# A third pause for every two scatters of gated copies, and a new weight for the stream that holds them

## The chip, the cores and the metric

The kernel runs on one core of a Trainium2 chip. The core has TensorE (PE: matmuls, with weight loads shown as PEld), VectorE (DVE), ScalarE (ACT), GpSimd (POOL) and SyncE (SP, which here only issues DMAs). Every engine works through its own instructions in order and waits on semaphores for the others. The metric is the time of one execution on the device in microseconds; the time of a kernel is the median of its runs.

## The reference, cut to what matters

Two layers over 16 x 256 tokens of 512 channels. The first is attention over blocks, a layer norm and a gated feed-forward in quantised weights; the second is a causal convolution over time, a router that picks two of eight experts for each token, and the experts.

```python
def _L0_ffn_ref(x, w1, w2, w3):
    h = jax.nn.silu(bitlinear(x, w1)) * bitlinear(x, w2)
    return bitlinear(h, w3)

def _L1_ffn_ref(x, Wr, We, be):
    logits = jnp.einsum('bsd,de->bse', x, Wr)
    w, sel = jax.lax.top_k(logits, K_TOP)          # K_TOP = 2
    w = jax.nn.softmax(w, axis=-1)
    E = We.shape[0]
    gate = jnp.einsum('bsk,bske->bse', w, jax.nn.one_hot(sel, E, dtype=w.dtype))
    out = jnp.zeros(x.shape[:2] + (We.shape[2],), dtype=x.dtype)
    for e in range(E):
        out = out + gate[..., e:e + 1] * (jnp.einsum('bsd,df->bsf', x, We[e]) + be[e])
    return out

x = x + _L0_ffn_ref(_L0_cond_ref(x, ...), L0_ffn_w1, L0_ffn_w2, L0_ffn_w3)
x = x + _L1_ffn_ref(_L1_cond_ref(x, cond_2048[:, None, :]), L1_ffn_Wr, L1_ffn_We, L1_ffn_be)
```

## The kernel before

**Tiling.** The 4096 tokens are cut into four blocks of 1024. A block is one tile of 128 partitions with eight rows of 512 channels in each (`X[n]`, two buffers, so that block n + 2 can be loaded only when block n is no longer read). The first layer goes row set by row set: 32 tiles m of 128 tokens, eight to a block.

**The streams.** Work is written as Python generators. Each `yield` is a pause: between two of them lies one step. The function `together` takes generators, each with a number of steps, and always advances the one whose share of steps done is smallest. So the number given with a generator is a weight: half the number makes it run twice as fast beside the others. It need not be its true number of steps.

- `ffn` is the first layer. A tile m takes six steps: four quarters of the gated product (`glu`: eight matmuls at L445, the SiLU at L450, the product at L451), after the first quarter a step with the down projection of tile m - 2 (`down`: sixteen matmuls at L487, L492), and a last step with the row quantisation (`quant_h`: L457, L459, L462, L463, with two small GpSimd operations at L359 and L131) and the transposes of the quantised rows (L475, copied by ScalarE at L477). The layer norm of two tiles at a time (L391 on GpSimd, L392 to L408, L414 to L419, turned at L427 and L429) is in there too. Its first tile of a new block is the first reader of that block.
- `behind(n - 1)` is the second layer's front for the block before: `conv`, `route`, and then the load of block n + 1 (`load_x`, four DMAs at L156 on SP).
- `experts` are the matmuls of full tiles of 128 rows for one expert each (turned at L983, multiplied at L1035), with rows read from `routed` in memory (L974) and results added into the output by GpSimd's indirect DMAs (L947). A tile takes three steps.

`conv` has ten steps (`CONV_STEPS`): two to begin, and then eight groups, each with the transposes (L675) and ScalarE's copy (L677) of the next group, 24 matmul instructions (L706) with weights loaded by SP (`taps`, L692, five buffers) and VectorE's copy of the result back into the block (L710). The accumulator comes from a pool of one bank (`ps_c`), in the tail from one of four (`ps_mm`).

`route` has nine steps of logits (transposes at L744, ScalarE's copy at L746, matmuls at L755), one with the choice of experts and of slots (L760 to L807, small operations of VectorE) and the table of tiles (`listing`), and then sixteen steps, one for each of eight rows and two chosen experts. Each of them makes a gated copy of the row (L819, ScalarE), appends four numbers (L823 on GpSimd, in the tail L821 on ScalarE) and scatters it by an indirect DMA from GpSimd (L824). The copies have three buffers (`pay`), in the tail they share twelve with other rows. In front of row 4 the table is multiplied out (L931) and cast (L936).

**The sections.** There are four. For n = 1, 2, 3 `behind(n - 1)` runs beside 48 steps (`STEPS`) of the first layer and, from n = 2 on, beside the experts of earlier blocks; n = 1 also has eight steps that load the experts' weights. In these sections `behind` is given `behind_steps * 7 // 4` as its weight, where `behind_steps = CONV_STEPS + ROUTE_STEPS` = 10 + 26 = 36. For n = 4, the tail, the first layer is done: convolution, logits and choice are stepped through without a partner, and the sixteen scatters run beside twelve tiles of experts (36 steps), with `behind_steps - head` as their number of steps, head being 20. Behind them come the last partial tiles of experts, which read rows of all scatters, and the final sum.

**The order.** What the streams set is the order in which instructions are written down. It is not yet the order on the engines: the instructions are then put in order by when they are ready as well, and the written order says which of several ready ones goes first.

## Time and profile before

| | us |
|---|---|
| median of 3 runs (lowest, highest) | 1011.78 (1010.33, 1012.91) |
| profiled execution | 1019.93 |
| its span, first to last instruction | 1018.0 |
| TensorE busy | 886.0 (87%) |
| VectorE busy | 570.2 (56%) |
| ScalarE busy | 484.1 (48%) |
| GpSimd busy | 315.6 (31%) |

The page gives busy times of the engines in the span, their shares of 40 equal slices, the costliest groups of instructions and the chain of work that ended last. A busy TensorE is not a TensorE at its peak, since matmuls are pipelined and their ends are modelled. The slices show where TensorE, ScalarE and GpSimd are busy, and the clock granted to TensorE:

```profile
PE   3678898798988899987998999879969998999992
...
ACT  2797765664577674456665515665511240111110
POOL 0135210323046312017434111462121045454541
PEclk9788998899999999999999999999989889999996
```

A slice is 25.45 us, a digit is tenths of it. The three sections lie at about 219 to 371, 371 to 561 and 561 to 747 us, the tail behind them. Of the groups, the scatters:

```profile
L824 POOL DMA_INDIRECT routed<-pay,slot x64 | 63.7, 995 | 42.6 <-issue 9.3
```

This reads: 64 instructions at line 824 on GpSimd, from `pay` and `slot` to `routed`, together 63.7 us busy, 995 ns in the mean, and GpSimd idle for 42.6 us in all just ahead of them.

### The profile page before, as it was taken

The page shows a single profiled execution, that of the slowest core. Times are in us where ns is not written, and L with a number is a line of the kernel's source. Part 1 is how long each engine was busy: PE and PEld are TensorE (multiplying, and loading weights), DVE is VectorE, ACT ScalarE, POOL GpSimd, SP SyncE. Part 2 cuts the span into 40 slices and gives each one's busy share as a digit, 9 for nine tenths or more (in the row PEclk, how much of TensorE's full clock was granted, in tenths as well). Part 3 has the DMA queues.
Part 4 walks back from the last instruction along what each step waited for, and adds up shares of the span by engine and source line. Part 5 has one row for each costly group of instructions (what it writes and reads, how often), then busy time and mean ns, then how long its engine had stood idle before and what let it go on. Part 6 is the DMA issues. An engine that isn't in the chain of part 4 may idle for free.

```text
span 1018.0 us, 13482 instructions
## 1 busy us (share of the span) xinstructions
PE 886.0 (87%) x4456; PEld 500.5 (49%) x4456; DVE 570.2 (56%) x1243; ACT 484.1 (48%) x635; POOL 315.6 (31%) x383
## 2 busy tenths in 40 slices
PE   3678898798988899987998999879969998999992
PEld 1223443357743467653443776435438944544440
DVE  3799864878385986454678543645513262333234
ACT  2797765664577674456665515665511240111110
POOL 0135210323046312017434111462121045454541
PEclk9788998899999999999999999999989889999996
DMA  9970100865226034325531642362579077877767
GB/s 331 356 263 0 60 21 7 283 230 159 63 84 225 26 102 157 95 66 173 166 84 19 191 146 63 105 197 63 109 221 273 17 216 214 219 176 193 180 162 241
DMA packets 73547, 151.56 MB, mean 149 GB/s; under 512 B 9276, under 2 KB 26044, under 8 KB 72840
## 3 DMA queue, kind: packets, MB, share of 16 engines
q1 hardware_dynamic: 57384, 108.93, 32.1%
q0 software_dynamic: 15440, 39.20, 16.3%
q10 hardware_dynamic: 656, 2.58, 0.8%
q8 instruction: 36, 0.59, 0.2%
q14 instruction: 31, 0.25, 0.1%
HBM read 96.50 MB, written 54.18 MB: 148 GB/s over the span
## 4 chain that ended last, share of the span: by engine, by line
PE 54%; DVE 13%; ACT 10%; DMA 9%; issue 7%; POOL 6%; SPq 0%; DVEq 0%; POOLq 0%; ACTq 0%
PE acc_ps L1035 19%; PE acc_ps L445 10%; PE acc_ps L706 7%; PE acc_ps L487 6%; PE acc_ps L755 3%; PE acc_ps L983 3%; DMA routed<-pay,slot 3%; ACT hq L457 2%; DVE h L451 2%; ACT hq L463 2%; PE acc_ps L744 2%; POOL routed L824 2%; DMA xg<-routed 2%; PE acc_ps L475 1%; DMA xt<-in_x 1%
## 5 line engine op out<-in xcount | busy, mean ns | idle before, releaser
L1035 PE MATMUL acc_ps<-we,xT 128*128 x568 | 267.3, 607 | 1.5 <-ACT h L450 1.3
L445 PEld LDWEIGHTS <-qT 128*128 128x128 bf16 x1024 | 99.6, 99 | 147.8 <-issue 42.8
L1035 PEld LDWEIGHTS acc_ps<-we,xT 128*128 128x128 f32 x568 | 105.7, 196 | 101.3 <-issue 94.7
L451 DVE SCALAR_TENSOR_TENSOR h<-acc_ps,c,h 128x512 f32<-128x512 f32 x128 | 95.2, 745 | 97.7 <-PE acc_ps L445 62.4
L445 PE MATMUL acc_ps<-w2q,qT 128*128 128x512 fp8e4 x512 | 133.6, 382 | 16.2 <-DVE h L451 8.5
L445 PE MATMUL acc_ps<-w1q,qT 128*128 128x512 fp8e4 x512 | 135.4, 384 | 8.4 <-ACT qT L429 4.1
L947 POOL DMA_INDIRECT out<-ye,oi x41 | 67.3, 1640 | 231.3 <-PE acc_ps L1035 145.4
L487 PE MATMUL acc_ps<-w3q,hqT 128*128 128x512 fp8e4 x512 | 130.2, 406 | 10.0 <-ACT w3q L217 4.6
L450 ACT ACTIVATE h<-acc_ps,c 128x512 f32<-128x512 f32 x128 | 86.3, 681 | 87.7 <-PE acc_ps L445 87.3
L986 ACT COPY xT<-acc_ps 128x512 f32<-128x512 f32 x59 | 34.4, 585 | 169.8 <-PE acc_ps L983 166.1
L706 PE MATMUL acc_ps<-taps,xT 128*128 128x128 f32 x768 | 93.1, 277 | 7.0 <-ACT xT L677 1.6
L706 PEld LDWEIGHTS acc_ps<-taps,xT 128*128 128x128 f32 x768 | 88.8, 192 | 9.9 <-ACT xT L677 2.0
L487 PEld LDWEIGHTS <-hqT 128*128 128x128 bf16 x512 | 52.3, 104 | 79.0 <-issue 26.9
L463 ACT ACTIVATE hq<-h,neg_magic 128x2048 bf16<-128x2048 f32 x32 | 64.1, 2002 | 32.7 <-DVE h L462 30.0
L824 POOL DMA_INDIRECT routed<-pay,slot x64 | 63.7, 995 | 42.6 <-issue 9.3
L459 DVE TENSOR_REDUCE hmx<-h 128x1 f32<-128x2048 f32 x32 | 73.0, 2281 | 0.6
L477 ACT COPY hqT<-acc_ps 128x1024 bf16<-128x1024 bf16 x64 | 61.9, 1009 | 17.9 <-PE acc_ps L475 16.4
L457 ACT ACTIVATE hq<-h 128x2048 bf16<-128x2048 f32 x32 | 61.2, 1912 | 16.8 <-DVE h L451 16.4
L983 PE MATMUL acc_ps<-ident,xg 128*128 128x128 f32 x284 | 45.7, 287 | 18.1 <-DMA xg<-routed 12.9
L1055 DVE SCALAR_TENSOR_TENSOR ye<-biases,xe,acc_ps 128x512 f32<-128x512 f32 x32 | 23.9, 747 | 66.3 <-PE acc_ps L1035 64.5
L983 PEld LDWEIGHTS acc_ps<-ident,xg 128*128 128x128 f32 x284 | 36.8, 150 | 45.3 <-issue 35.7
L359 POOL TENSOR_SCALAR ms<-hss 128x1 f32<-128x1 f32 x32 | 6.2, 192 | 170.0 <-ACT hq L457 169.4
(194 smaller groups left out, 1134.4 us busy)
## 6 DMA issues: line engine op xcount, KB each, us to landing
taps<-in_toep SPq DMA_DIRECT2D x128, 192.0 KB, 2.7
xg<-routed SPq DMA_DIRECT2D x71, 258.0 KB, 3.2
xt<-in_x SPq DMA_DIRECT2D x16, 512.0 KB, 8.2
we<-in_We SPq DMA_DIRECT2D x8, 1024.0 KB, 10.8
bias<-in_be SPq DMA_DIRECT2D x25, 256.0 KB, 4.0
out<-xt SPq DMA_DIRECT2D x12, 512.0 KB, 2.6
st<-in_w1T SPq DMA_DIRECT2D x4, 1024.0 KB, 12.5
st<-in_w2T SPq DMA_DIRECT2D x4, 1024.0 KB, 14.4
```

The lines of the kernel that those rows point to most:

```text
L445: nc.tensor.matmul(acc[-1], lhsT=qTs[i][:, k, bass.ts(j, P)], rhs=wq[:, k, bass.ts(f, 512)], start=(k == 0), stop=(k == KC - 1),)
L450: marks["silu", m] = nc.scalar.activation(h, acc[0], AF.Silu, scale=c1[:, j : j + 1])
L451: marks["glu", m] = nc.vector.scalar_tensor_tensor(h, acc[1], c2[:, j : j + 1], h, ALU.mult, ALU.mult)
L457: nc.scalar.activation(hq, h, AF.Square, accum_out=hss)
L459: nc.vector.tensor_reduce(hmx, h, AX.X, ALU.max, apply_absolute_value=True)
L463: nc.scalar.activation(hq, h, AF.Identity, bias=neg_magic)
L487: nc.tensor.matmul(o_ps, lhsT=hqT[k // half][:, k % half, :], rhs=w3q[:, k, :], start=(k == 0), stop=(k == KF - 1),)
L706: nc.tensor.matmul(cv_ps[:, g, :], lhsT=xT[:, g, at : at + P], rhs=mine[g][:, lag, :], start=(lag == 0), stop=(lag == LAGS - 1),)
L824: routings.append(nc.gpsimd.indirect_dma_start(out=next(rv), out_offset=bass.IndirectOffsetOnAxis(ap=slot[:, i, p : p + 1], axis=0), in_=p ...
L947: d = nc.gpsimd.indirect_dma_start(out=next(add_v), out_offset=bass.IndirectOffsetOnAxis(ap=idx, axis=0), in_=ye, in_offset=None, compute_ ...
L983: nc.tensor.transpose(xT_ps[:, k, :], xg[:, bass.ts(k, P)], ident)
L1035: last_mm = nc.tensor.matmul(e_ps, lhsT=xT[:, k, :], rhs=we[:, bass.ds(e, 1), k, :].rearrange("p o f -> p (o f)"), start=(k == 0), stop=(k ...
```

## The change

After both scatters of a row there is one more pause. So a row has three steps where it had two, in one of which nothing is issued. `ROUTE_STEPS` counts it: 26 becomes 34. Through it `behind_steps` goes from 36 to 44, its weight in the three sections from 63 to 77, and the number of steps of the scatters in the tail from 16 to 24. No instruction is added, removed or altered.

```diff
--- before.py
+++ after.py
@@ -827,7 +827,9 @@
                 ))
                 yield
 
-    ROUTE_STEPS = 1 + PH + 1 + TOP * PH
+            yield
+
+    ROUTE_STEPS = 1 + PH + 1 + (TOP + 1) * PH
```

## The prediction

> **What bounds the kernel now.** I read the page's engine shares first (TensorE busy 87%), then the times of the scatters (L824): 290.9 to 320.6, 457.3 to 488.6, 651.7 to 681 and, in the tail, 825.5 to 857.2 us. With them as boundaries I asked for the busy time of each engine by stretch. For the first of the three sections that run the first layer beside the second, and the two last stretches of the third section:

> ```profile
> core 0: us, PE busy (x) PEld busy (x) DVE busy (x) ACT busy (x) POOL busy (x), PEclk, DMA share, GB/s
> 219.00:280.00 61.00, 57.78 (x446) 46.68 (x446) 36.38 (x61) 31.32 (x42) 11.53 (x14) 1.00 0.44 139
> 280.00:322.00 42.00, 34.88 (x201) 17.49 (x202) 28.82 (x83) 33.75 (x45) 23.56 (x41) 0.96 0.33 124
> 322.00:371.00 49.00, 43.03 (x233) 20.98 (x232) 42.43 (x88) 34.15 (x44) 16.31 (x26) 0.97 0.19 67
> ...
> 641.00:683.00 42.00, 35.41 (x165) 17.60 (x166) 23.12 (x94) 28.41 (x39) 25.02 (x40) 0.92 0.49 152
> 683.00:747.00 64.00, 63.78 (x306) 31.95 (x304) 31.07 (x56) 30.40 (x35) 13.79 (x14) 1.00 0.41 94
> ```

> Convolution and logits (219 to 280) keep TensorE at 95% with ScalarE at 51%; the scatters (280 to 322) leave TensorE 7.1 us idle while ScalarE is at 80%; here the two trade places. TensorE's waits in 280 to 322 name ScalarE first:

> ```profile
> PE acc_ps L427 <- ACT hqT L477: 3.7, 2, 3.1
> PE acc_ps L445 <- DVE h L451: 1.8, 2, 1.0
> PE acc_ps L445 <- ACT h L450: 1.1, 2, 0.9
> ```

> What ScalarE does there beside the first layer is the gated copy (L819, 16 x 0.716 us = 11.1 us in a section). Its three buffers come back only when a scatter has landed; of the scatters' row, who waited for them:

> ```profile
> who waited for it (us, times):
>   ACT pay L819: 23.0, 21
> ```

> ScalarE works in order, so each such wait (16.5 us in the three sections, the rest in the tail) holds the first layer's L450 and L477 behind it. In the chain that ended last, the first section's scatters also hold the next block of x:

> ```profile
> 316.26 2.75 DMA routed<-pay,slot
> 319.12 0.73 ACT pay L819
> 319.87 5.91 DMA xt<-in_x
> ```

> The last copy frees the block, its successor is loaded at once, and GpSimd's L391 at 326.0 had waited 2.46 us for it (0.99 in the second section).

> [...] By the busy row the three scatter stretches lose 42.0-34.88, 43.0-34.96 and 42.0-35.41, in all 21.8 us. [...] I therefore multiplied the matmuls of each stretch by the undisturbed start-to-start distance of their kind in this trace (0.216 us for L445 and L487, 0.056 for L475, 0.112 for L706, 0.429 for L1035): needed 32.1, 32.4 and 31.4 us, lost 9.9, 10.6 and 10.6, in all 31.1. The same count gives 17.1 us lost in 217 us of convolution and logits (8%), and 19.6 in 183 us behind the scatters (10.7%). I use the counted figures; by the busy row the stretches behind lose 13.2 of 184 us (7.2%), the excess below would be 12.7 us, and the gain at the scatters 2.1 us in place of 2.9.

> **The change, part by part.** It adds no instruction: it moves priorities in the round-robin. The stream of the second layer is weighted by 36*7//4 = 63 before and 44*7//4 = 77 after, beside 48 steps of the first layer: 0.762 and 0.623 first-layer steps per step. A first-layer tile is 6 steps and 32 L445, 16 L487, 16 L475 and half of 8 L427 matmuls, 11.5 us, so a step is 1.92 us of TensorE.

> *Convolution and logits* are the first 20 steps: they should be through at step 15.24 before and 12.47 after, 2.77 steps or 5.3 us earlier. *Scatters* spread from 15.24-26.67 to 12.47-26.18, from 11.4 to 13.7 steps, so 20% thinner. *The load of the next x* is called at 36/63 = 44/77 = 0.571, the same place. The table's matmul and cast (L931, L936) move from 28/63 to 32/77, 1.4 steps earlier; they take under 0.5 us on their engines, and nothing waits for them in the traced stretch.

> (a) Scatters. At the 10.7% of the stretches behind them, 127 us would lose 13.6; the excess is 31.1-13.6 = 17.5 us. Copies at 1/1.2 of the density take a sixth off it: 2.9 us. Bounds: nothing, if the copies keep to their buffers' pace anyway; 5.8 us if all waits for landings go and the copies stay (16.5 of the 16.5 + 33.5 us that both fill on ScalarE, a third of the excess). I take -2.9. [...]

> (b) Next x. Copies that start 5.3 us sooner end sooner, unless the longer spread takes it back. The waits of 2.46 and 0.99 us bound the gain at 3.4; the first is on the chain. I take -2.5. What is late next is ScalarE's L463.

> (c) Convolution and logits lose cover. 16 hand-overs per section (eight of one accumulator bank to VectorE's 1.03 us copy L710, eight of transposes to ScalarE's 0.585 us copy L746) now have 1.46 us of first-layer work between them, then 1.20.

> ```profile
> L710 DVE COPY xt<-acc_ps x32: 1009/1032/1064, 224.5 to 795.8; 128x512 f32<-128x512 f32 x32
> ```

> Only what has no other matmul to put in the gap pays. TensorE's waits here are few: 3.1 us for L746 in the second section, 1.8 in the third, none there in the first. Between nothing and 48 x 0.27 = 12.8 us I take +1.5, near the row, as eight waits with 6.4 us in all name these two copies (the rest of the second and third section's are of 0.2 to 0.7 us). The DMAs go along: 32 loads of taps (192 KB each, on SP behind L706's release of five buffers) in a stretch shorter by a tenth; one wait of 1.4 us for taps stands in the third section, and may double. GpSimd's queue also carries the adds (L947, 1.6 us) and the norm's small steps (L359, L131): a scatter moved ahead of one delays it by 1 us, one that now stands behind it gives that back.

> (d) First-layer work pushed behind: under half a step net per section, 0.5 x 1.92 x 10.7% x 3 = 0.3 us; inside (c)'s margin.

> (e) Tail. Sixteen scatters go beside 36 expert steps; the second of each pair moves from 2.25 to 1.5 steps behind the first, the last of all from step 33.75 to 33. A tile takes 3.87 us, a step 1.29: 0.97 us sooner. TensorE stands 4.6 us there:

> ```profile
> 857.17 2.72 DMA routed<-pay,slot
> 860.57 3.79 DMA xg<-routed
> ```

> Between 0 and -1.0 I take -0.5, since GpSimd's adds may keep the order.

> Sum: -2.9 -2.5 +1.5 -0.5 = -4.4 us. The profiled execution took 1019.93 us (span 1018.0 and 1.9 outside), 0.8% above the median 1011.78; the share is 0.43%, so I forecast 1007.4 us.

> **Rivals.** *The pauses have no hold* (about 1011.5). Order on the engines isn't the traced order, so what is ready runs ahead:

> ```profile
> 283.43 0.44 POOL L823 COPY pay<-ends 128x4 f32<-128x4 f32 x3 [15.25 <-DVE ends L774]
> 290.89 1.22 POOL L824 DMA_INDIRECT routed<-pay,slot  x1 [7.03 <-DVE hit L850]
> ```

> The code has each L824 between two L823; three L823 ran first. In the tail ScalarE made 12 copies from 818 to 827 us, though their turns are spread over 32 us. Counting L450 on ScalarE, the copies run at first-layer steps 18 to 24 in the third section (turns 15.2 to 26.7) and 18 to 30 in the first, where the landings set the pace. Then (a) and (e) vanish, and what (b) gains (c) takes back. Against it: copies and L450 compete on ScalarE at 80%, where turn does decide.

> *The mixed stretch gets thinner* (slower, 1018). [...] If a hand-over in the order finds VectorE in L459 (2.28 us), it costs up to 2.28+1.03 us less the 0.66 us of transposes. With (c) at +9 (of 12.8) and (a), (b), (e) at half, -3, the sum is +6. It decides once the 48 hand-overs lose more than 5.9/48 = 0.12 us each on average. For it: one bank only (ps_c), and the waits for L746 are already there. Against: in the tail, convolution with no first layer runs at 3.13 us a group with 0.5 us idle in 27.

> **How the numbers follow.** A change under about 0.3% (3 us) can't be told from none here. Forecast 0.46 (near 1007, nearly all faster), no hold 0.22 (near 1011.5), thinner mix 0.32 (near 1018). Spilling at the edges gives faster 0.46, same 0.22, slower 0.32. Lower end: (a) -5.8, (b) -3.4, (e) -1 and (c) 0 make -10.2, 1001.6; a new order of instructions elsewhere may add as much as one such wait. Upper end: the thinner mix with (c) at its bound and little else, +10, 1021. The forecast's own range is 1001 to 1009.

> **What would show it.** Right: first copies some 5 us sooner in each section (283.4 before in the first), fewer than 16.5 us of ScalarE waiting for landings there, L391 no longer waiting for x. Wrong in (c): TensorE's waits for L710 and L746 growing from 6.4 us. No hold: sixteen scatters still take 30 to 34 us per section at a spacing of about 2 us. The forecast fails if the convolution doesn't move up at all, because TensorE already takes what is ready there.

## The result, and the profile after

The changed kernel took 1042.89 us (median of four runs, 1040.79 to 1050.60) beside 1012.35 for the kernel before (four runs, 1010.33 to 1014.08): 1.0288 times the time, with a 95% interval of 1.0244 to 1.0332. It is slower by about 30 us, where 1007.4 was forecast and 1021 was the upper end of the range.

The profiled execution took 1041.7 us. The head of its page (span, then busy time, share of the span and instructions of each engine):

```profile
span 1039.7 us, 13476 instructions
PE 890.3 (86%) x4456; PEld 504.6 (49%) x4456; DVE 571.6 (55%) x1243; ACT 483.1 (46%) x635; POOL 318.3 (31%) x383
```

The counts of instructions (of 13482, six fewer) and nearly all busy times are those of before; the 21.7 us of span that have come are not new work. The same stretches as in the prediction, after (columns as there; code behind L829 stands two lines lower in this kernel, so L983 and L1035 are L985 and L1037):

```profile
core 0: us, PE busy (x) PEld busy (x) DVE busy (x) ACT busy (x) POOL busy (x), PEclk, DMA share, GB/s
217.00:285.00 68.00, 62.63 (x466) 50.02 (x467) 38.98 (x75) 31.68 (x44) 10.52 (x15) 0.97 0.40 125
285.00:323.00 38.00, 28.79 (x169) 14.12 (x168) 23.96 (x69) 31.65 (x43) 22.47 (x38) 0.99 0.34 127
323.00:378.00 55.00, 46.92 (x247) 22.67 (x246) 44.74 (x91) 35.68 (x45) 18.97 (x28) 0.93 0.19 67
...
662.00:708.00 46.00, 38.14 (x169) 18.86 (x168) 25.47 (x92) 30.14 (x42) 27.46 (x44) 0.89 0.51 153
```

Convolution and logits of the first section left TensorE 3.2 us idle before (61 less 57.78) and leave it 5.4 now (68 less 62.63); the scatters left 7.1 and leave 9.2; the stretch behind them left 6.0 and leaves 8.1. The clocks of 0.93 and 0.89 in the last two rows show a second loss.

TensorE's waits over the whole run (the instruction that waited, what it waited for, us in total, times, the longest):

```profile
PE acc_ps L445 <- ACT h L450: 14.6, 11, 2.9
PE acc_ps L445 <- DVE h L451: 13.6, 11, 3.5
...
PE acc_ps L706 <- DVE xt L710: 5.8, 4, 3.2
PE acc_ps L706 <- issue: 5.7, 2, 3.7
```

Before, the four read 9.1, 10.5, 0.7 and 0.6 us. The matmuls of the convolution (L706) now wait 11.5 us in these two rows instead of 1.3 (both are waits for the bank, as the timeline below shows), and those of the first layer's gated product (L445) 28.2 instead of 19.6.

**An account that holds for every kernel here.** I took the time from the first copy L677 of the first section to that of the tail (three sections; the third ends at 770.4 us before and 796.7 after), added up TensorE's gaps of more than 150 ns, and the time at a granted clock of 0.5; the clock in this trace is either 1.0 or 0.5, and at 0.5 the matmuls start about twice as far apart (those of L445 0.427 us instead of 0.216, those of L706 0.213 instead of 0.112). Section time less the gaps less half of the half-clock time is the same in all 17 profiles, 477 to 483 us, which is the work itself:

| | three sections | TensorE gaps | time at half clock | rest |
|---|---|---|---|---|
| before | 550.7 | 55.5 | 30.7 | 479.8 |
| after | 579.0 | 71.2 | 58.0 | 478.7 |

So the 28.3 us are 15.7 us of new gaps and 13.7 us for 27.3 us more at half clock, less 1.1 of the rest. The tail, 247.7 and 243.0 us, has no part in them; it is shorter as it has 20.8 us at half clock in this profile and 34.3 in that of before. This split isn't one profile's luck. What half clock takes from a whole run is (1 - mean clock) x span; averaged over the runs it is 50 us for before (the 25 beside the first experiments) and 62 for after (four), and what is left of the span is 963 and 980 us.

By stage (convolution to the last L710 of a section, logits to the first gated copy, scatters to the end of the last L824), against the undisturbed distances between matmuls that the prediction used, convolution lost 10.6 us before and 25.5 after (its gaps 7.0 and 16.2); logits 10.8 and 6.4; scatters 26.5 and 31.9; what lies behind them 31.7 and 44.1.

**Where the convolution stands still.** The timeline of after around one of its gaps (start, duration, engine, line, operation, output and input; in brackets the idle time of the engine before it and its releaser):

```profile
409.07 1.03 PE L487 MATMUL acc_ps<-w3q,hqT 128*128 128x512 fp8e4 x4
409.36 1.42 DVE L406 SCALAR_TENSOR_TENSOR y<-y,mv,gamma 128x512 f32<-128x512 f32 x2
409.49 0.68 POOL L399 TENSOR_SCALAR ve<-mv 128x2 f32<-128x2 f32 x1 [1.62 <-DVE mv L393]
410.25 1.09 POOL L131 TENSOR_TENSOR rstd<-ve,neg_half 128x2 f32<-128x2 f32 x1
411.38 1.42 DVE L407 SCALAR_TENSOR_TENSOR y<-y,rstd,beta 128x512 f32<-128x512 f32 x2 [0.60 <-POOL rstd L131]
412.71 1.00 DVE L710 COPY xt<-acc_ps 128x512 f32<-128x512 f32 x1
...
413.81 2.55 PE L706 MATMUL acc_ps<-taps,xT 128*128 128x128 f32 x14 [3.72 <-issue]
```

The matmuls of the group before ended at 408.8, so the result could have been copied then. But L710 stands in VectorE's queue behind L406 and L407 of the layer norm, and L407 waits for GpSimd's reciprocal root (L399, L131) until 411.3. VectorE is idle for only 0.60 us of this; the rest is its own work. The copy starts at 412.7, and the one bank comes free 4.9 us after it was full. TensorE has only four matmuls of L487 and four transposes to put there; 3.72 us are left empty. The label "issue" hides this: the wait is for the bank, and the next L706 starts 0.1 us behind the copy's end. This is the gap of the second section; the first has one of 1.94 us (ended 250.0) and the third one of 3.18 (ended 619.9), and in all three L710 follows L407 and L407 the same chain over GpSimd.

The late copy is not new. The same hand-over in the second section of before:

```profile
396.86 3.62 PE L487 MATMUL acc_ps<-w3q,hqT 128*128 128x512 fp8e4 x16
397.60 1.42 DVE L406 SCALAR_TENSOR_TENSOR y<-y,mv,gamma 128x512 f32<-128x512 f32 x2
399.60 1.42 DVE L407 SCALAR_TENSOR_TENSOR y<-y,rstd,beta 128x512 f32<-128x512 f32 x2 [0.59 <-POOL rstd L131]
400.31 1.88 PE L1035 MATMUL acc_ps<-we,xT 128*128 x4
400.93 1.04 DVE L710 COPY xt<-acc_ps 128x512 f32<-128x512 f32 x1
402.03 0.60 PE L675 MATMUL acc_ps<-ident,xt 128*128 128x128 f32 x4
```

There too the bank comes free 5.0 us after it was full (at 397.0), behind the same L406 and L407. But TensorE had all sixteen matmuls of a down projection and four of the experts for that time, and no gap. Over the three sections these late hand-overs kept the bank for 3.5, 5.0 and 5.0 us before and 2.9, 4.9 and 4.7 after; TensorE had 12.0 us of other matmuls in them before and has 3.9 now. Its idle time there went from 2.1 to 8.8 us, most of what the convolution's gaps grew by. What the change took away is the cover of the one late hand-over in each section.

**What follows such a gap.** The gap of after by windows, columns as above, the clock being the one in front of the last two:

```profile
408.70:413.80 5.10, 1.40 (x9) 0.67 (x9) 4.50 (x9) 0.59 (x1) 1.77 (x2) 1.00 0.55 170
413.80:414.70 0.90, 0.89 (x8) 0.90 (x9) 0.90 (x1) 0.00 (x0) 0.00 (x0) 0.98 0.55 201
414.70:418.10 3.40, 3.40 (x19) 3.40 (x18) 0.05 (x1) 0.00 (x0) 0.00 (x0) 0.50 0.41 116
418.10:421.50 3.40, 3.40 (x16) 1.73 (x16) 1.53 (x2) 0.00 (x0) 0.00 (x0) 1.00 0.44 121
```

From 0.9 us behind the gap TensorE runs for 3.4 us at half clock, and loses another 1.7 us while it shows as fully busy. Each of the three gaps has such a window (from 250.8, 414.7 and 619.5 us; the last begins inside its gap). All half-clock stretches in the three sections of these two traces are 3.41 us long or a multiple of it: nine such windows before and seventeen after.

### The profile page after: what moved, and what is told of

It is laid out like the page before. It is cut to its first block, busy times and chain, and to the rows that moved or that the text cites. A ratio compares the mean times of both kernels' runs of the same rounds, so it can differ in the third digit from the quotient of the medians.

```text
span 1039.7 us, 13476 instructions
## 1 busy us (share of the span) xinstructions
PE 890.3 (86%) x4456; PEld 504.6 (49%) x4456; DVE 571.6 (55%) x1243; ACT 483.1 (46%) x635; POOL 318.3 (31%) x383
## 3 DMA queue, kind: packets, MB, share of 16 engines
q1 hardware_dynamic: 57384, 108.93, 32.1%
## 4 chain that ended last, share of the span: by engine, by line
PE 52%; DVE 15%; ACT 11%; issue 7%; DMA 7%; POOL 7%; SPq 0%; DVEq 0%; POOLq 0%; ACTq 0%
PE acc_ps L1037 17%; PE acc_ps L445 10%; PE acc_ps L706 7%; PE acc_ps L487 6%; DMA routed<-pay,slot 3%; PE acc_ps L755 3%; PE acc_ps L985 3%; ACT hq L457 2%; ACT hq L463 2%; DVE h L451 2%; ACT hqT L477 2%; DMA xg<-routed 2%; DVE h L462 1%; PE acc_ps L475 1%; POOL r L131 1%
## 5 line engine op out<-in xcount | busy, mean ns | idle before, releaser
L1037 PE MATMUL acc_ps<-we,xT 128*128 x568 | 264.9, 602 | 1.0 <-ACT h L450 0.8
L445 PEld LDWEIGHTS <-qT 128*128 128x128 bf16 x1024 | 100.3, 100 | 159.8 <-issue 55.2
L445 PE MATMUL acc_ps<-w2q,qT 128*128 128x512 fp8e4 x512 | 137.4, 389 | 22.9 <-DVE h L451 13.0
L1037 PEld LDWEIGHTS acc_ps<-we,xT 128*128 128x128 f32 x568 | 104.3, 193 | 98.2 <-issue 92.2
L451 DVE SCALAR_TENSOR_TENSOR h<-acc_ps,c,h 128x512 f32<-128x512 f32 x128 | 95.0, 745 | 99.3 <-PE acc_ps L445 48.5
L445 PE MATMUL acc_ps<-w1q,qT 128*128 128x512 fp8e4 x512 | 138.1, 387 | 10.9 <-ACT h L450 4.9
L450 ACT ACTIVATE h<-acc_ps,c 128x512 f32<-128x512 f32 x128 | 86.1, 681 | 116.0 <-PE acc_ps L445 115.8
L487 PE MATMUL acc_ps<-w3q,hqT 128*128 128x512 fp8e4 x512 | 128.1, 399 | 8.8 <-ACT w3q L217 5.1
L988 ACT COPY xT<-acc_ps 128x512 f32<-128x512 f32 x59 | 34.4, 585 | 170.1 <-PE acc_ps L985 167.1
L706 PE MATMUL acc_ps<-taps,xT 128*128 128x128 f32 x768 | 98.0, 286 | 15.9 <-DVE xt L710 5.8
L706 PEld LDWEIGHTS acc_ps<-taps,xT 128*128 128x128 f32 x768 | 93.8, 200 | 20.8 <-issue 7.1
L487 PEld LDWEIGHTS <-hqT 128*128 128x128 bf16 x512 | 51.6, 102 | 75.3 <-issue 20.6
L463 ACT ACTIVATE hq<-h,neg_magic 128x2048 bf16<-128x2048 f32 x32 | 64.0, 2001 | 41.2 <-DVE h L462 38.6
L824 POOL DMA_INDIRECT routed<-pay,slot x64 | 65.5, 1023 | 40.9 <-issue 10.0
L459 DVE TENSOR_REDUCE hmx<-h 128x1 f32<-128x2048 f32 x32 | 73.0, 2280 | 0.4
L457 ACT ACTIVATE hq<-h 128x2048 bf16<-128x2048 f32 x32 | 61.2, 1912 | 21.8 <-DVE h L451 21.5
L477 ACT COPY hqT<-acc_ps 128x1024 bf16<-128x1024 bf16 x64 | 61.9, 1009 | 16.6 <-PE acc_ps L475 16.5
L359 POOL TENSOR_SCALAR ms<-hss 128x1 f32<-128x1 f32 x32 | 6.1, 192 | 197.8 <-ACT hq L457 197.1
L985 PE MATMUL acc_ps<-ident,xg 128*128 128x128 f32 x284 | 44.6, 281 | 19.4 <-DMA xg<-routed 13.3
L1057 DVE SCALAR_TENSOR_TENSOR ye<-biases,xe,acc_ps 128x512 f32<-128x512 f32 x32 | 23.9, 746 | 63.8 <-PE acc_ps L1037 61.3
L985 PEld LDWEIGHTS acc_ps<-ident,xg 128*128 128x128 f32 x284 | 36.0, 146 | 47.0 <-issue 36.2
## 6 DMA issues: line engine op xcount, KB each, us to landing
we<-in_We SPq DMA_DIRECT2D x8, 1024.0 KB, 10.7
st<-in_w1T SPq DMA_DIRECT2D x4, 1024.0 KB, 13.3
```

The costliest lines, as they stand in the source:

```text
L445: nc.tensor.matmul(acc[-1], lhsT=qTs[i][:, k, bass.ts(j, P)], rhs=wq[:, k, bass.ts(f, 512)], start=(k == 0), stop=(k == KC - 1),)
L450: marks["silu", m] = nc.scalar.activation(h, acc[0], AF.Silu, scale=c1[:, j : j + 1])
L451: marks["glu", m] = nc.vector.scalar_tensor_tensor(h, acc[1], c2[:, j : j + 1], h, ALU.mult, ALU.mult)
L457: nc.scalar.activation(hq, h, AF.Square, accum_out=hss)
L459: nc.vector.tensor_reduce(hmx, h, AX.X, ALU.max, apply_absolute_value=True)
L463: nc.scalar.activation(hq, h, AF.Identity, bias=neg_magic)
```

## The experiments

To pace parts of the stream by themselves, I gave it the weight 693 = 11 x 63 and let inner step k take so many turns; 11 is the pace of before (48/63 first-layer steps a step), 9 that of after (48/77). The load of x stays at turn 396 of 693, where both kernels have it (395 in e15).

```diff
+    def pace(k):
+        return 9 if k < 20 else 51 if k == 35 else 11
+
+    def paced(it):
+        for k, _ in enumerate(it):
+            for _ in range(pace(k)):
+                yield
...
-            streams = [(behind_steps * 7 // 4, behind(n - 1, ps_c, "conv"))]
+            streams = [(693, paced(behind(n - 1, ps_c, "conv")))]
```

Steps 0 to 9 are the convolution, 10 to 18 the logits, 19 the choice, 20 to 35 the scatters. What is longer or shorter than before is made up behind the last scatter. The runs, with the account of their profiled executions (us; before is 55.5 and 30.7):

| run | ratio to before, 95% interval | gaps | half clock |
|---|---|---|---|
| e2_pauses_only | 0.9984 (0.9951 to 1.0017) | 54.4 | 27.3 |
| e3_tail_only | 0.9955 (0.9915 to 0.9996) | 56.2 | 27.3 |
| e1_front_only | 1.0167 (1.0109 to 1.0225) | 62.4 | 44.4 |
| e4_front_half | 1.0101 (1.0063 to 1.0140) | 63.3 | 37.5 |
| e11_conv_only | 1.0109 (1.0024 to 1.0194) | 64.5 | 44.4 |
| e12_logits_only | 1.0031 (0.9984 to 1.0079) | 53.3 | 54.6 |
| e8_front_slow | 1.0141 (1.0071 to 1.0212) | 60.7 | 47.8 |
| e13_weight_64 | 1.0079 (1.0029 to 1.0129) | 56.2 | 37.5 |
| e5_after_copy_act | 1.0218 (1.0137 to 1.0300) | 61.6 | 47.8 |
| e6_before_copy_act | 1.0027 (0.9990 to 1.0063) | 52.5 | 37.5 |
| e16_front_act | 1.0092 (1.0059 to 1.0124) | 55.7 | 41.0 |
| e9_after_two | 1.0212 (1.0150 to 1.0274) | 67.2 | 54.6 |
| e10_front_dense | 1.0267 (1.0176 to 1.0358) | 66.7 | 75.1 |
| e14_front_pairs | 1.0204 (1.0161 to 1.0248) | 61.3 | 58.0 |
| e15_front_even_long | 1.0292 (1.0243 to 1.0341) | 69.8 | 51.2 |

### The parts of the change alone

**The denser front** (pace as in the diff above):

> Before, with convolution and logits at 9/693 of the stream per step (48/77 of a first-layer step each, as in after) and the scatters at 11/693 each without a third pause (as in before), the load of the next x at its old place, the tail as before. Theory F (a denser front loses its cover: the hand-over of the one convolution bank): about +25 to +32 us against before, most of it lost in the convolution stretch and behind the scatters. Theory S (thinner scatters are what costs): within 4 us of before. Theory O (any new order of instructions is worse than the one before): +10 to +35.

1.0167: more than half of the loss comes from the first 20 steps alone. That is 18 us, less than theory F expected, and inside O's wide range, so this run alone doesn't tell the two apart. L706 waits 7.1 us for L710 and 5.7 under "issue", the same stops as in after. The stretches behind the scatters lose only as much as before: their gaps are 21.6 us (21.5 before, 29.1 after).

**The pauses in the scatters:** `return 11 if k < 20 else 15 if k % 2 else 7`

> Before, with the front at its old pace of 11/693 per step and each pair of scatters at turns 0 and 7 of 22 (a third pause), in the same total, the tail as before. The planned order on TensorE and VectorE is that of before. F: within 3 us of before. S: +10 us or more. O: within 3 us of before, since TensorE keeps its order.

No change. In the traces TensorE and VectorE run the same instructions in the same order as before; 6 places of ScalarE's order and 10 of GpSimd's differ. Pairs and pauses hardly reach the engines, as the ready work is taken in its own order.

**The pause in the tail:** the third `yield` under `if pool == "tail"`, and `behind_steps - head + PH` as the number of steps.

> Before, with the third pause in the tail alone (24 steps beside the experts' 36), the three sections untouched. F and S: 0 to -5 us (the tail of after took 243.0 us against 247.7). O: slower than before by several us.

In the traces the order on TensorE, VectorE, ScalarE and GpSimd is identical to before's, so this run is a second measurement of the same program. Its ten runs spread from 1004.57 to 1021.77, and its ratio, 0.9955 with an interval up to 0.9996, shows that a ratio here can be off by some 0.4%. Step (e) is worth nothing.

**Half of the front:** `return 10 if k < 20 else 31 if k == 35 else 11`

> As the front-only kernel, with convolution and logits at 10/693 per step, half way between before (11) and after (9). F: about half of its cost, +10 to +16 us. S: within 4 us. O: a jump of its own size, not half: as much as the front-only kernel or more, or nearly none.

1.0101: more than half of the front's loss, and about half of its stops (L706 waits 2.8 us for L710, 3.1 under "issue"). Its gaps, 63.3 us, are no fewer than those of the full front: L445 waits 18.8 us for L450 here (10.3 there). So the loss doesn't follow the stops on the bank alone.

**The front cut in two:** `return 9 if k < 10 else 13 if k < 20 else 11`, then `return 11 if k < 10 else 9 if k < 20 else 31 if k == 35 else 11`

> Before, with only the convolution's ten steps denser (9/693 each, as in after) and the logits' ten thinner (13/693), so that choice, scatters and the load of x have the turns of before. Theory H (the bank's hand-over behind the layer norm): the convolution stalls of about 1.9, 3.7 and 3.2 us on L710 are there, TensorE idles 7 to 10 us more in the three convolution stretches than before, and the time is 8 to 15 us above before. Theory D (displaced first-layer work): what the convolution gives away the logits take back, within 4 us of before.

> Before, with only the logits' ten steps denser (9/693) and the convolution at its old pace; the scatters start 20/693 earlier and keep their spacing, the load of x keeps its place. H: no stalls on L710 in the convolution, and less than half of the front-only kernel's cost: 0 to 8 us above before. D: half of it or more, 8 to 12 us.

The convolution alone costs 1.0109, and its stops come back (6.2 us for L710, 5.6 under "issue"). The logits alone cost 1.0031, which can't be told from nothing; their late hand-overs have the cover of before (TensorE is idle for 5.4 us in all hand-overs of the convolution, as before; 14.8 in after). Both are as theory H expected, though the lower end of the first interval, 1.0024, doesn't exclude D.

### The bank of the convolution

**The copy on another engine,** in after, and then in before:

```diff
-            nc.vector.tensor_copy(grouped[:, c * G4 : (c + 1) * G4, :], cv_ps)
+            nc.scalar.copy(grouped[:, c * G4 : (c + 1) * G4, :], cv_ps)
```

> After, with the copy out of the convolution's one bank (L710) moved from VectorE to ScalarE, where no layer-norm chain stands in front of it; TensorE's planned order is nearly that of after. Theory H (the bank's hand-over behind the layer norm on VectorE is what the dense front costs, together with the half-clock windows that follow its stalls): the stalls of 1.9, 3.7 and 3.2 us on that bank go, convolution loses about 11 us in place of 25.5, and the time falls by 10 to 17 us against after, to some 1.013 of before. Theory D (first-layer work displaced out of the mixed stretch is what costs): the stalls go, but the stretches behind keep their loss, and the time falls by less than 6 us against after.

> Before, with the same move of L710 to ScalarE; TensorE keeps its order but for ten places. The convolution of before waits for L710 for 1 us in all, so both theories: within 4 us of before (0.996 to 1.004). If it is faster by more, the move is a gain of its own, and as much has to be taken off what the same move brings in after.

The convolution's loss falls from 25.5 to 14.2 us, near the 10.6 of before, but the kernel only from 1.0288 to 1.0218, less than H expected; the intervals overlap. The stretches behind keep most of their loss (39.3 us; 44.1 in after), as D expected. Over all runs the span without what half clock takes falls from 980 to 972 us, but half clock still takes 63 us (62 in after). In before the same edit gains nothing: there L710 stands behind the layer norm just as late, but TensorE has other work for that time.

**The same in the kernel with the early front alone** (e1_front_only with L710 on ScalarE):

> The front-only kernel with L710 on ScalarE. Theory H: the three convolution stalls go (9 us of idle time and the half-clock windows behind them), so 8 to 13 us below the front-only kernel, at 1.004 to 1.009 of before. If the stalls go and the time stays within 4 us of the front-only kernel, the hand-over was not its cost.

1.0167 becomes 1.0092: 10 us between the medians (1033.92 and 1023.48). The intervals touch (from 1.0109, and up to 1.0124), but the slowest of these seven runs, 1024.54, is below the fastest of the front alone, 1026.85. The gaps fall by 6.7 us, all of them in the convolution (17.3 to 10.1 us there). L710 in this run (duration, what its engine waited for, who waited for it):

```profile
L710 ACT COPY xt<-acc_ps x32: 994/1036/1070, 222.2 to 802.2; 128x512 f32<-128x512 f32 x32
...
  PE acc_ps L706: 61.5, 26
...
  PEld acc_ps L706: 11.7, 14
  PE acc_ps L706: 7.1, 14
```

The copy takes the same 1.04 us, its engine waits for nothing but L706 ahead of it, and TensorE waits for it 14 times by 0.5 us on average, where the front alone had four of 1.8 us and two more of 2.9 under "issue". So it is not the copy's price that costs, but what stands in front of it in its engine's queue when TensorE has nothing else to run. The edit isn't quite a single change: 88 of the 4456 places in TensorE's order differ from the front alone.

**Two banks instead of one** (after, with `ps_c` of two banks and `ps_mm` of three):

> After, with two accumulator banks for the convolution, the second taken from the first layer's four. H: TensorE no longer waits for L710 in the convolution (11 us in all in after, with the weight loads' waits), some 10 us off after, less what the first layer loses by its bank. D: no gain, or slower than after by what the bank costs.

No wait for L710 is left, yet 1.0212; that is below after, with intervals that overlap. Now the weights are late, and the first layer has one bank less; of TensorE's waits in this run:

```profile
PE acc_ps L706 <- DMA taps<-in_toep: 9.8, 5, 3.1
```

The taps, waited for 1.5 us in after, cost 9.8, and L445 waits 34.4 us for its banks instead of 28.2. A second bank taken from the first layer moves much of the wait elsewhere.

### What is left: the scatters behind an early front

**A slower front:** `return 12 if k < 20 else 21 if k == 35 else 9`

> Before, with the front slower: convolution and logits at 12/693 per step (before 11, after 9), the scatters at 9/693, the load of the next x at its old place. D: more first-layer work beside the convolution, so faster than before by 3 to 8 us, the other side of the slope of the two denser fronts. H: no hand-over to win in the convolution, within 4 us of before. A theory of luck (any order but the one before is worse): slower by 8 us or more.

1.0141, slower, where D expected a gain and H no change. Both missed; the theory of luck, slower by 8 us or more, came true. So "denser" is not simply the bad direction: the pace of before loses on both sides. The trace shows part of it: the late hand-overs of the second and third section are there again, with three and two matmuls of L487 under them, and TensorE's idle time in the hand-overs is 9.5 us (5.4 before). The larger part, some 9 us by the clocks of all runs, is half clock.

**The next weight:** 64 in place of 63 in the kernel before, nothing else.

> Before, with the stream's weight 64 in place of 63 and nothing else: the smallest step in the direction of after (convolution and logits 0.75 of a first-layer step each in place of 0.762). H and D: within 3 us of before, a tenth of the way to after. Theory O (the order of before is a lucky one, its neighbours are all worse): 5 us or more above before.

1.0079, again a miss of H and D and as theory O expected. A change of 1.6% in one weight costs 8 us (3 to 13 by the interval). L706 waits 5.1 us under "issue" (0.6 before), 2.9 of them at once: the late hand-over of the first section now has four matmuls of L445 under it in place of eight.

**Scatters as dense as can be:** `return 9 if k < 20 else 216 - 15 * 7 if k == 35 else 7`

> The front-only kernel (front at 9/693) with the scatters packed at 7/693 each in place of 11, the load of x at its old place. If thinner scatters behind an early front cost what after has beyond the front-only kernel (1.0288 against 1.0167), then denser ones are faster than the front-only kernel by some 5 us (about 1.012). If the turns of the scatters decide nothing, it is within 4 us of the front-only kernel.

A miss: 1.0267, slower than the front alone and not faster. The gaps are only 4 us over those of the front alone; it is the half-clock time, 75.1 us, that is the longest of all. The intervals of the two overlap.

**Pause without length, length without pause.** First `9 if k < 20 else 55 if k == 35 else 15 if k % 2 else 7`: pairs with a pause, no longer than before. Then `9 if k < 20 else 13 if k == 35 else 14 if k % 2 else 13`: as long as in after, evenly spread.

> The front-only kernel (front at 9/693) with its scatters in pairs, each pair at turns 0 and 7 of 22, so with after's pause but in the front-only kernel's length. Its planned order on TensorE is that of the front-only kernel. Theory L (the length of the scatters behind an early front decides, not the pause): as the front-only kernel, 1.010 to 1.022 of before. Theory P (the pause between pairs costs): as after, 1.024 or more.

> The front-only kernel with its scatters evenly spaced at 13.5/693, as long as after's scatters with their pauses, but without any pause between pairs. The planned order of all five engines is then that of after. L: as after, 1.024 to 1.034 of before. P: as the front-only kernel, below 1.023.

The second gives 1.0292 against 1.0288 for after, and in its trace TensorE, VectorE and ScalarE run in after's order: the pause adds nothing, and what after has beyond the front alone comes with the length of its scatters. The first gives 1.0204, with an interval that overlaps that of the front alone (1.0167), and TensorE's order is that of the front alone; the two are two measurements of nearly one program. The waits of L445 in the evenly long kernel (14.6 and 13.3 us) are after's, to 0.3 us; the front alone has 10.3 and 11.0. By place, all of the growth is behind the scatters: L445 waits there for 6.2 us in the front alone (6.5 before), and for 14.0 and 14.2 in the two kernels with long scatters.

## Why the prediction was wrong

Two of its steps failed most. Step (c) was right in its mechanism, lost cover, but much too small; step (a) has the wrong sign. Together they make the 28.3 us of the sections: 10.5 in convolution and logits, 17.8 in the scatters and behind them. The second rival, the mixed stretch that gets thinner, was right for its place and near in size (10.5 us instead of 9), but no rival had the second loss. By the prediction's steps:

- **(c) was mis-sized.** Convolution and logits were to lose 1.5 us more, 12.8 at most. The convolution lost 14.9 more (25.5 less 10.6), the logits 4.4 less. The step reasoned with the average cover of a hand-over, 1.20 us instead of 1.46. But cover isn't lost evenly. Of the eight groups of a section most hand over in good time, and one gets its bank back only after 3 to 5 us, in both kernels. Before, the work under these three was 12.0 us; it became 3.9, and TensorE stops there for 1.9 to 3.7 us each. The rival named the right resource, one bank and VectorE's queue, but the wrong blocker: L459 (2.28 us) instead of L406, L407 and the wait between them. One argument against the rival didn't hold: the tail's convolution shows little idle time with no first layer beside it, but it draws on four banks there. That the hand-over is what costs is shown by the edit on ScalarE: 10 us back in the front alone, and 6 between the medians in after, there with intervals that overlap.
- **(a) has the wrong sign.** Scatters and the stretches behind were to gain 2.9 us; they lost 17.8 (76.0 less 58.2). The scatters' density was thought to be the cost. From first to last scatter a section now takes 33 to 37 us (31 to 32 before), but ScalarE's waits for landings in the sections are 18.3 us (16.5 before), so the thinner spread freed no buffers sooner. (A section's 16 copies of 0.716 us are 11.5 us; the 11.1 of the prediction is their busy time, in which neighbours overlap.) Nor did the copies come earlier throughout: counted from the start of its section, the first one is 3.6 us later in the first, 0.9 earlier in the second and 5.5 earlier in the third. The larger part of the loss, 12.4 of the 17.8 us, is behind the scatters, a stretch that the step took as its undisturbed measure: new gaps of L445 (6.5 to 14.2 us) and 12.6 us more at half clock.
- **(b) gave nothing in the first section.** Its load starts at 321.8 us, before at 319.9; GpSimd's L391 then waits 2.33 us for it, before 2.46. Only the wait in the second section (0.99 us before) is gone.
- **(d) was put at 0.3 us, inside (c)'s margin.** The first layer's matmuls in convolution and logits, counted at the same distances, fell from 78.2 to 70.2 us over the three sections, and those of the experts from 27.2 to 22.0. Of these 13.2 us, 10.8 moved beside the scatters and 2.5 behind them. The first layer's 8 us are more than the half step net per section (2.9 us) that the step counted, but at its rate of 10.7% they are still under 1 us; the rate, not the amount, is what missed.
- **(e)** gave nothing, as the order of the tail is unchanged.
- **What the sum had no term for:** half clock. 13.7 of the 28.3 us come as slower matmuls, in which TensorE counts as busy. The profile of before already had 30.7 us of it in the three sections, and the clocks of 0.96 and 0.92 stood in the rows that the prediction shows.

The first rival, the pauses without a hold, was right of the pauses themselves: e2, e3 and e15 show that pairs and pauses hardly reach the engines. What reached them was the weight, 77 in place of 63.

**Shown and not shown.** Shown by an edit: the bank's hand-over in the early convolution, some 10 us of the front's 17. Shown by the traces: what made it cost is the missing work under it. Shown by reproduction: the early front alone is 1.0167 and 1.0204 in two measurements, and with the longer scatters behind it the whole 1.0292. Not settled: why this length gives an order with more gaps of L445, and the last 0.9% of e16. Longer and denser scatters both lose, a slower front loses too, and the weight beside 63 loses 0.8%. This fits an order of before that happens to put work under all three late hand-overs, where the orders of e1, e4, e8 and e13 leave at least one with a gap of 2.8 us or more; for the convolution the traces show it, for the stretches behind the scatters it is argued. More buffers for the gated copies weren't tried. No version is clearly faster than before.

## What to carry to other kernels

Where a stage has a single accumulator bank, don't price the hand-over by its mean cover. Find the one hand-over that is late, by looking at what stands in the copying engine's queue ahead of the copy, and then at what the matmul engine has to run in that time, before and after the change. In the second section a late copy with 5.5 us of matmuls under it cost nothing; the same copy with 1.3 us under it cost 3.7 us. Price each gap of TensorE with the half-clock window that may follow it (here 3.41 us, of which 1.7 are lost). And in a kernel whose order is made by readiness, test whether a pause changes the order at all before pricing it; a weight changes the whole order, and one weight further on can cost a quarter of the effect that is argued about.

## What the runs showed of the hardware

How much half clock a program gets is not fixed by its order. The 25 runs of before beside the first four experiments went from 1009.58 us (mean clock 0.958) to 1021.90 (0.939), and e3, the same program, went down to 1004.57 (0.962). The kernel with the logits alone moved, with gaps of 53.3 us, fewer than before, had 54.6 us at half clock in its profile, and its ratio is 1.0031. So a ratio here needs many runs, and a single profile's half-clock sum must not be read as its kernel's.
